# Channel statistics in three terms per chunk, two more blocks for ScalarE, and later pooled sums on GpSimd

## The chip, the cores and the metric

The kernel runs on one core of one Trainium2 chip. The metric is the device time of one execution in microseconds (us). TensorE is called PE, VectorE DVE, ScalarE ACT, GpSimd POOL; SP is the engine that only issues DMAs.

## The reference

The input x has 384 channels of 192 x 192 pixels, fp32. Two layers follow each other, each adding to x what it makes of the group-normalised x (32 groups of 12 channels):

```python
def _gn(v, G=32, eps=1e-5):
    g = v.reshape(B_, G, C_ // G, H_, W_)
    m = jnp.mean(g, axis=(2, 3, 4), keepdims=True)
    s = jnp.var(g, axis=(2, 3, 4), keepdims=True)
    return ((g - m) / jnp.sqrt(s + eps)).reshape(v.shape)

x = x + _L0_conv_ref(_gn(x), ...)   # 1x1 conv to q, k, v; 2x2 max; 3x3 depthwise;
                                    # channel attention; gelu; upsample by 2; 1x1 conv
x = x + _L1_conv_ref(_gn(x), ...)   # seven depthwise convs (13x13 and six smaller), each
                                    # with a batch norm, summed
```

The change concerns the first `_gn`: the mean and variance of each group of x, which must be known before the first 1x1 convolution can be finished.

## The kernel before

**Stages.** Channels are held as three chunks of 128 partitions (j = 0, 1, 2). The first stage, up to about 172 us, reads the whole of x once for its statistics. Then comes the main loop of 432 steps: `project` (L615, PE) multiplies a strip of x by the weights of one output chunk, `pool` takes the 2x2 maximum (L627 DVE, L634 ACT), and nine depthwise taps follow (L663 DVE). After it come the attention product with gelu, the second 1x1 convolution, and the large convolution (L1297).

**The statistics loop.** The first rows of all chunks arrive in the large tiles `xts` (read by L381 and L382). The rest of a chunk is cut into NX = 22 blocks of 128 x 1536 values (768 KB), and the loop runs over n = 22 j + b, 66 blocks in all, in a schedule written by hand (`manual_schedule`): within it each engine gets its instructions in the order in which the program issues them. A block is measured in one of two ways.

- By DVE: three `bn_stats` of 512 values (L476), each of which writes six numbers into `stats[:, j]`.
- By ACT, for the blocks b in BY_ACT = (4, 7, 10, 13, 16, 19) of chunks 0 and 1: the block plus a pivot with its sum (L472), and the square of that with its sum (L473), each followed by a short read of the accumulator. The pivot is the negative mean of the chunk's first block (L483, L484). The sums go to `acc`.

At the last block of a chunk (b = 21), after its L476, one `bn_aggr` (L505) makes mean and variance of all of the chunk's `stats`, and L510 to L515 do so for `acc`. Groups of 12 channels don't divide 128, so a few channels of the next chunk (`spares`) are measured as well (L502, L503) for chunks 0 and 1. Each of these results is a column of `mvx`; seven columns exist.

`group_stats` joins columns into groups: `mean_of` (L112) multiplies each column by its weight matrix `gw[k]` and adds up in PSUM, L123 spreads the group means back over the channels (one product for each term), L127 to L129 form the deviations, a second `mean_of` the variance, and L147 spreads scale and shift, which end up in `gn0`. It is a generator: with `apart` its steps are placed one by one between L476 instructions. It runs three times: `ga` for chunk 0 within chunk 1, `ge` for chunk 1 within chunk 2, and `g0` for chunk 2 after the loop.

**Loads.** Blocks land in a ring of eight buffers (eight more blocks, `kept`, have places of their own). `load_blocks` is called after each block: the buffer just read is given back and at once taken by the next block that waits, which is block n + 8 for n of 26 and more. It is issued from POOL if its number is odd and from SP if it is even:

```python
                eng = nc.scalar if n < 8 else nc.gpsimd if n % 2 == 1 else nc.sync
                eng.dma_start(out=xs, in_=x[j * P : (j + 1) * P, FX + b * FB : FX + (b + 1) * FB])
```

**Early products.** As soon as a chunk's `gn0` is known, PE starts on 18 products (EARLY). `first_chunk` advances by a step at each L476 of chunk 1, `early` at each L476 of chunk 2 until it first yields True (`going`). ACT prepares their input (`ready`, L387), copies results out of PSUM (`put_by`, L409) and earlier partial results back into PSUM (`fill`, L246). `early` first goes through `group_stats`, then, without a yield, through its entries 0 to 14, and yields at entry 15 and after. Each `ready` also appends its input to `early_sums`; `sum_one`, called at every odd n, makes POOL add up four pixels to one (L257 to L259) and store the result with a DMA (L261). What is left of `early_sums` is done after the loop, ahead of the main loop. There are 16 such sums.

`merge`, one step for each n, has POOL merge the convolution weights and prepare `gw`. L1029 to L1035, written after the main loop in a section of their own that runs partly beside it (they execute near 1607 us), combine columns of `mvx` into the input's variance `mv0` for the second normalisation.

Of the kernel before, what the change touches and what calls it, by code (L numbers as in the profile page):

```python
# [7 lines left out]
F32 = mybir.dt.float32  # L8
AF = mybir.ActivationFunctionType
ALU = mybir.AluOpType  # L10
AX = mybir.AxisListType
# [3 lines left out]
P = 128  # L15
# [5 lines left out]
NG = 32  # L21
# [36 lines left out]
def tile_attn_then_large_kernel_conv(ctx: ExitStack, tc: tile.TileContext, a: dict, out: bass.AP):  # L58
# [118 lines left out]
    mv0 = const.tile([P, NJ, 2], F32, name="mv0")  # L177


    mvx = const.tile([P, 7, 2], F32, name="mvx")  # L180
    BY_ACT = (4, 7, 10, 13, 16, 19)
    PART = len(BY_ACT) * R / HS
    PARTS = (1 - PART, PART)
    terms = [(0, NJ), (1, 0), (2, 0), (3, NJ + 1), (4, 1), (5, 1), (6, 2)]
    ctx_v, ctx_a, ctx_qk = ExitStack(), ExitStack(), ExitStack()
    vpool = ctx_v.enter_context(tc.tile_pool(name="vpool", bufs=1))
    v = vpool.tile([P, NJ, HS, WS], F32, name="v")
# [80 lines left out]
    with (  # L268
# [60 lines left out]
            out=wd[:, :nqk], in_=a["w_dw"][: nqk * P].rearrange("(m p) t -> p m t", p=P)  # L329
        )  # L330
        nc.gpsimd.dma_start(out=bdw[:, :nqk], in_=a["b_dw"][:, :nqk])
        gwt = s1.tile([P, 2 * NJ - 2, NG], F32, name="gw")
        gw = []
        for j in range(2):

            e = stats[:, j].rearrange("p n s -> p (n s)")
            gw += [e[:, -3 * NG : -2 * NG], gwt[:, 2 * j], gwt[:, 2 * j + 1]]
        gw.append(gm[:, 2])

        def merge():  # L340

            c0 = BC - 1
            for j in range(NJ):
                nc.gpsimd.tensor_scalar(wf[:, j, c0 : c0 + K0, :], wbs[0][:, j], scale[:, j, 0:1], None, ALU.mult)
                yield
                for i, (k, r) in enumerate(BRANCHES):
                    o = PAD - r * (k - 1) // 2
                    n = r * (k - 1) + 1
                    zv = wf[:, j, c0 + o : c0 + o + n : r, o : o + n : r]
                    wb = wbs[i + 1][:, j]  # L350
                    nc.gpsimd.tensor_scalar(wb, wb, scale[:, j, i + 1 : i + 2], None, ALU.mult)
                    nc.gpsimd.tensor_add(zv, zv, wb)
                    yield
                if j > 0:
                    continue
                for jj in range(2):
                    g = P * (jj + 1) // CG
                    nc.gpsimd.memset(gw[3 * jj], 0.0)
                    nc.gpsimd.memset(gw[3 * jj][:, g : g + 1], MORE[jj] / P / CG)
                    for q, part in enumerate(PARTS):  # L360
                        nc.gpsimd.tensor_scalar(gw[3 * jj + 1 + q], gm[:, jj], part, None, ALU.mult)
                    yield
                    k = P * (jj + 1) - 1
                    nc.gpsimd.tensor_copy(
                        gmt[:, C + jj * P : C + (jj + 1) * P], gmt[:, k : k + 1].to_broadcast([NG, P])
                    )
                    yield
# [42 lines left out]

        def first_chunk():

            pc = yield from group_stats(s1, s_ps, mvx, "ga", gw, terms[:3], (0,), True)
            yield
            nc.vector.tensor_copy(gn0[:, 0], pc[:, 0])
            yield
            blocks = sorted({B for B, _ in EARLY if B >= NKEEP})
            ready(blocks[0], 0, 0)
            for B, m in EARLY:
                if B < NKEEP:  # L420
                    continue
                ps = multiply(B, m, (0,))
                if m == 0 and B + 1 in blocks:
                    ready(B + 1, 0, 0)
                if m > 0 and B - NKEEP < 2 * NKEEP // (NJ - 1) and m < NJ:
                    n = (B - NKEEP) * (NJ - 1) + m - 1
                    ready(n // 2, n % 2, 0)
                put_by(B, m, ps)
                yield
                yield  # L430

        def early():

            pc = yield from group_stats(s1, s_ps, mvx, "ge", gw, terms[1:6], (1,), True)
            yield
            nc.vector.tensor_copy(gn0[:, 1], pc[:, 1])
            ready(0, 0, 1)
            ahead = None
            for n, (B, m) in enumerate(EARLY):
                if m == 0 and B < EARLY[-1][0]:  # L440
                    ready(B + 1, 0, 1)
                ps = multiply(B, m, (0, 1)) if B < NKEEP else multiply(B, m, (1,), ahead)
                if n + 1 < len(EARLY) and EARLY[n + 1][0] >= NKEEP:
                    fill(*EARLY[n + 1], 0)
                    ahead = filled.pop()
                if n == len(EARLY) - 1:
                    yield True
                put_by(B, m, ps)
                if n < NKEEP:
                    ready(n, 1, 1)  # L450
                if n >= len(EARLY) - LATE - 1:
                    yield True
# [5 lines left out]
        early_sums, pieces = [], {}  # L458
        begin, first = first_chunk(), early()
        going = False  # L460
        pivot = s1.tile([P, 2, 2], F32, name="pivot")
        acc = s1.tile([P, 2, len(BY_ACT), 2], F32, name="acc")
        done = [NS0] * NJ
        for n in range(NJ * NX):
            if n in (1, 3, 5, 7):
                rows_stats(n // 2)
            j, b = divmod(n, NX)
            xt = xss.pop(n)
            if j < 2 and b in BY_ACT:

                sums2 = acc[:, j, BY_ACT.index(b)]
                nc.scalar.activation(xt, xt, AF.Identity, bias=pivot[:, j, 0:1], accum_out=sums2[:, 0:1])  # L472
                nc.scalar.activation(xt, xt, AF.Square, accum_out=sums2[:, 1:2])  # L473
            else:
                for q in range(FB // 512):
                    nc.vector.bn_stats(stats[:, j, done[j], :], xt[:, q * 512 : (q + 1) * 512])  # L476
                    done[j] += 1
                    if j == 1:
                        next(begin, None)
                    if j == 2 and not going:  # L480
                        going = next(first)
                if j < 2 and b == 0:
                    nc.vector.bn_aggr(pivot[:, j], stats[:, j, NS0 : done[j]].rearrange("p n s -> p (n s)"))  # L483
                    nc.vector.tensor_scalar(pivot[:, j, 0:1], pivot[:, j, 0:1], -1.0, None, ALU.mult)  # L484
            if (j, b) not in kept:
# [1 line left out]
            for _ in load_blocks():  # L487
                pass
            next(merging, None)
            if n % 2 == 1:  # L490
                sum_one()
            if j < 2 and b == NX - 16:
                w = P * (j + 1)
# [4 lines left out]
            if j < 2 and b == NX - 6:  # L498
                k = HW * MORE[j] // P // 384
                sy = stats[:, j, -k:]  # L500
                for q in range(k):
                    nc.vector.bn_stats(sy[:, q, :], spares[j][:, q * 384 : (q + 1) * 384])  # L502
                nc.vector.bn_aggr(mvx[:, 3 * j, :], sy.rearrange("p n s -> p (n s)"))  # L503
            if b == NX - 1:
                nc.vector.bn_aggr(  # L505
                    mvx[:, (1, 4, 6)[j], :], stats[:, j, : done[j]].rearrange("p n s -> p (n s)")
                )
                if j < 2:
                    m = mvx[:, 3 * j + 2, :]
                    nc.vector.tensor_reduce(m, acc[:, j].rearrange("p n s -> p s n"), AX.X, ALU.add)  # L510
                    nc.vector.tensor_scalar(m, m, 1.0 / len(BY_ACT) / FB, None, ALU.mult)
                    t = s1.tile([P, 1], F32, name=f"sq{j}")
                    nc.vector.tensor_mul(t, m[:, 0:1], m[:, 0:1])
                    nc.vector.tensor_sub(m[:, 1:2], m[:, 1:2], t)
                    nc.vector.tensor_sub(m[:, 0:1], m[:, 0:1], pivot[:, j, 0:1])  # L515
        nc.sync.dma_start(out=wqk[:, 2, :C], in_=wqkv[:, 2, :C])
        nc.sync.dma_start(out=wqk[:, :, C:], in_=wqkv[:, :, C : 2 * C])
        nc.sync.dma_start(
            out=wfd.rearrange("(j p) s -> p j s", p=P), in_=wf.rearrange("p j x y -> p j (x y)")
        )  # L520
        last = group_stats(s1, s_ps, mvx, "g0", gw, terms[4:], (2,))
        for _ in range(5):
            next(last)
        next(first)
# [5 lines left out]
        normalize(0, 1, 2)  # L530
        next(first)
        assert next(first, first) is first


    mv1 = const.tile([P, NJ, 2], F32, name="mv1")
# [4 lines left out]
    with ctx_v:  # L540
# [362 lines left out]
        def gram_next():  # L903
            add_gram(*turned.pop(0))

        attention = []

        def begin_attention():
# [10 lines left out]
            for u in range(2 * NJ if B >= NB else 4 * NJ)  # L919
        ]  # L920
        with ctx_m:
            for sb in range(2):
                for j in range(NJ):
                    normalize(0, sb, j)
                    add_up(0, sb, j)
# [60 lines left out]
        with (  # L986
# [31 lines left out]
            with tc.manual_schedule():  # L1018
# [5 lines left out]
                nc.vector.tensor_mul(t, t, gn0[:, :, 1])  # L1024
                nc.vector.tensor_sub(pre[:, :, 0], bpj, t)
                nc.vector.memset(mv1, 1.0)

                d = b1.tile([P, 2, 1], F32, name="d")
                nc.vector.tensor_sub(d, mvx[:, 1:5:3, 0:1], mvx[:, 2:6:3, 0:1])  # L1029
                nc.vector.tensor_mul(d, d, d)  # L1030
                nc.vector.tensor_scalar(d, d, PART * (1 - PART), None, ALU.mult)
                for q, part in enumerate(PARTS):
                    nc.vector.scalar_tensor_tensor(d, mvx[:, q + 1 : q + 5 : 3, 1:2], part, d, ALU.mult, ALU.add)
                nc.vector.tensor_copy(mv0[:, :2, 1:2], d)
                nc.vector.tensor_copy(mv0[:, 2, 1:2], mvx[:, 6, 1:2])  # L1035
                hxs = [gather(b) for b in range(2)]
                sms = [load_sums(b) for b in range(2)]
                for c in range(NJ):
# [468 lines left out]
```

## Time and profile before

| | us |
|---|---|
| median of 3 runs (3071.37 to 3073.4) | 3073.17 |
| the profiled execution | 3071.29 |
| its span in the trace | 3069.2 |
| PE, DVE, ACT, POOL busy | 2934.8, 2516.2, 1336.9, 933.6 |
| first load to the first L615 | 0.75 to 174.68 |
| first block of chunk 0, 1, 2 begun by DVE | 11.59, 70.60, 121.42 |
| `gn0` written for chunk 0, 1, 2 | 78.23, 129.84, 172.07 |
| last block issued, landed, aggregated | 155.00, 163.18, 167.26 |
| main loop (first to last L615) | 174.68 to 1919.9 |

The page divides the span into 40 slices, gives the busy share of each engine in tenths, and follows the work that ended last back to the start (the chain of waits). In a timeline, a line gives the start, the busy time, the engine, the line of the program, the operation with output and input, the count, and in brackets how long the engine had been idle before it and what released it.

### The profile page before, as it was taken

What the parts mean: (1) busy time and instruction counts of PE and PEld (TensorE: products, weight loads), DVE (VectorE), ACT (ScalarE), POOL (GpSimd) and SP (SyncE); (2) the same over time, 40 slices, a digit from 0 to 9 for tenths busy, and PEclk for the clock granted to TensorE, in tenths of its full rate; (3) what the DMA queues carried; (4) which work ended last, traced back from release to release, by engine and by line L of the source; (5) the groups of instructions that cost most, each with busy time, mean ns of one, the idle gap of its engine ahead of it and who ended that gap; (6) DMA issues with size and microseconds to landing.
All of it is one profiled execution on the core that took longest, in us unless ns stands there. A gap on an engine that the chain in (4) does not pass through costs nothing.

```text
span 3069.2 us, 32213 instructions
## 1 busy us (share of the span) xinstructions
PE 2934.8 (96%) x10842; PEld 1943.7 (63%) x10842; DVE 2516.2 (82%) x3483; ACT 1336.9 (44%) x2457; POOL 933.6 (30%) x1147
## 2 busy tenths in 40 slices
PE   0699999999999999999999999999999999999998
PEld 0355556666666666665555555555777777777776
DVE  6778897888878787879999999888788777777775
ACT  2655554444444444444444444733333333333332
POOL 4422133232323242412222222500333333333332
PEclk9899999999999999999999999999999999999999
DMA  9943342434333333433333332577999999999994
GB/s 386 381 155 105 121 155 85 146 96 138 102 128 112 122 124 109 138 104 103 102 101 110 124 102 70 179 225 205 264 266 242 247 240 246 246 244 245 244 219 119
DMA packets 275924, 525.73 MB, mean 171 GB/s; under 512 B 25954, under 2 KB 190480, under 8 KB 275632
## 3 DMA queue, kind: packets, MB, share of 16 engines
q1 hardware_dynamic: 204432, 326.44, 39.8%
q0 software_dynamic: 49376, 174.29, 17.6%
q10 hardware_dynamic: 21952, 22.95, 2.2%
q8 instruction: 86, 1.41, 0.2%
q14 instruction: 78, 0.64, 0.1%
HBM read 362.23 MB, written 161.37 MB: 171 GB/s over the span
## 4 chain that ended last, share of the span: by engine, by line
PE 83%; DVE 10%; DMA 3%; issue 2%; ACT 1%; POOL 0%; ACTq 0%; SPq 0%; POOLq 0%; DVEq 0%
PE qkv L615 45%; PE conv L1297 29%; DVE v L663 3%; PE pj L1359 3%; DVE acc L663 2%; PE av L1051 2%; DVE mx L627 2%; PE gram L704 2%; PE tr L692 2%; DMA v<-in_x 1%; DMA xt<-in_x 1%; PE qkv L398 1%; DVE stats L476 1%; DMA smj<-sums 1%; DMA pd<-pjs 1%
## 5 line engine op out<-in xcount | busy, mean ns | idle before, releaser
L615 PE MATMUL qkv<-xt,wqk 128*128 128x384 f32 x3312 | 1088.6, 487 | 5.6 <-ACT qkv L246 5.1
L1297 PE MATMUL conv<-xp,wt 128*128 128x288 f32 (+1 forms) x3840 | 919.4, 403 | 2.2 <-ACT co L1305 2.2
L615 PEld LDWEIGHTS qkv<-xt,wqk 128*128 128x128 f32 x3312 | 621.6, 190 | 425.7 <-ACT qkv L246 11.5
L1297 PEld LDWEIGHTS conv<-xp,wt 128*128 128x128 f32 x3840 | 730.1, 190 | 189.2 <-ACT co L1305 2.6
L663 DVE SCALAR_TENSOR_TENSOR acc<-pooled,wd,acc 128x384 f32<-128x384 f32 (+2 forms) x1152 | 731.9, 635 | 30.6
L634 ACT ACTIVATE pooled<-mx,bq 128x192 f32<-128x192 f32 x432 | 197.1, 456 | 922.0 <-DVE mx L627 921.8
L627 DVE TENSOR_REDUCE mx<-qkv 128x192 f32<-128x768 f32 x432 | 412.3, 954 | 211.5 <-PE qkv L615 199.0
L1279 DVE STREAM_TRANSPOSE xp<-xn 128x4608 f32<-128x4608 f32 (+1 forms) x107 | 441.9, 4130 | 172.8 <-PE conv L1297 163.3
L615 PE MATMUL qkv<-xt,wv 128*128 128x384 f32 x1728 | 563.7, 487 | 1.7 <-ACT xt L596 1.1
L615 PEld LDWEIGHTS qkv<-xt,wv 128*128 128x128 f32 x1728 | 325.5, 190 | 234.4 <-ACT xt L596 7.5
L1305 ACT ACTIVATE co<-conv,cb 128x288 f32<-128x288 f32 x384 | 191.4, 499 | 602.4 <-PE conv L1297 592.1
L663 DVE SCALAR_TENSOR_TENSOR v<-pooled,wd,v 128x384 f32<-128x384 f32 (+2 forms) x576 | 375.7, 652 | 15.1
L257 POOL TENSOR_TENSOR sum<-xt 128x192 f32<-128x192 f32 x128 | 87.3, 682 | 957.0 <-ACT xt L596 944.4
L1322 POOL DMA_DIRECT2D out<-o x191 | 106.1, 585 | 571.7 <-DVE o L1313 514.1
L596 ACT ACTIVATE xt<-xt,gn 128x768 f32<-128x768 f32 x278 | 275.8, 1016 | 0.0
L1256 POOL TENSOR_TENSOR raw<-raw,up 128x2496 f32<-128x2496 f32 x46 | 230.9, 5019 | 23.3 <-DMA up<-pd 23.0
L1313 DVE STREAM_TRANSPOSE o<-co 128x2304 f32<-128x2304 f32 (+1 forms) x50 | 209.8, 4200 | 19.8 <-ACT co L1305 19.8
L732 POOL DMA_DIRECT2D zd<-v x96 | 72.2, 759 | 242.1 <-ACT v L723 241.4
L1359 PE MATMUL pj<-v,wp 128*128 128x384 f32 x432 | 142.5, 488 | 0.9 <-ACT gx L1062 0.6
L1359 PEld LDWEIGHTS pj<-v,wp 128*128 128x128 f32 x432 | 81.0, 190 | 55.5 <-ACT gx L1062 1.2
L258 POOL TENSOR_TENSOR sum<-sum,xt 128x192 f32<-128x192 f32 x128 | 100.9, 788 | 10.8
L1264 ACT ACTIVATE xn<-raw,par 128x2112 f32<-128x2112 f32 x48 | 102.9, 2143 | 1.2 <-ACT pjs L1367 1.2
(284 smaller groups left out, 1918.7 us busy)
## 6 DMA issues: line engine op xcount, KB each, us to landing
xt<-in_x SPq DMA_DIRECT2D x96, 1152.0 KB, 7.5
wt<-zd SPq DMA_DIRECT2D x46, 1536.0 KB, 13.4
raw<-in_x SPq DMA_DIRECT2D x182, 312.0 KB, 13.1
out<-o POOLq DMA_DIRECT2D x188, 288.0 KB, 6.7
zd<-v POOLq DMA_DIRECT2D x96, 416.0 KB, 4.6
up<-pd SPq DMA_DIRECT2D x184, 156.0 KB, 12.2
xs<-in_x POOLq DMA_DIRECT2D x20, 768.0 KB, 10.0
smj<-sums SPq DMA_DIRECT2D x72, 192.0 KB, 2.9
```

The source lines that it names most:

```text
L596: nc.scalar.activation(xt[:, j], xt[:, j], AF.Identity, bias=gn0[:, j, 1:2], scale=gn0[:, j, 0:1])
L615: nc.tensor.matmul(ps[:, r, : 2 * W], lhsT=wq[:, j, mm * P : (mm + 1) * P], rhs=xt[:, j, r * 2 * W : (r + 1) * 2 * W], start=(j == 0), sto ...
L627: nc.vector.tensor_reduce(mx, ps[:, :, : 2 * W].rearrange("p r (y w x) -> p r w y x", y=2, x=2), AX.XY, ALU.max,)
L634: nc.scalar.activation(pool_t[m][:, k : k + SR, 1 : 1 + WS], mx, AF.Identity, bias=bq[:, m : m + 1])
L663: nc.vector.scalar_tensor_tensor(acc[:, :nt], pool_t[m][:, k0 + dy : k0 + dy + nt, dx : dx + WS], wd[:, m, t : t + 1], acc[:, :nt], ALU.mu ...
L1256: eng.tensor_add(rv, rv, uv.unsqueeze(2).to_broadcast([P, (m1 - m0) * WS, 2]))
L1279: nc.vector.transpose(bass.AP(at.tensor, at.offset, [list(at.ap[0]), [NBQ, n], [1, NBQ], [NQ * NBQ, CC], [ME * NBQ, NE]],), bass.AP(row.te ...
L1297: nc.tensor.matmul(ps[:, t0:t1], lhsT=wt[:, c, o : o + P], rhs=d[:, c, g + 2 * t0 : g + 2 * t1 - 1 : 2, :], start=(g == 1), stop=(g == NGR ...
L1305: nc.scalar.activation(co[:, c], ps, AF.Identity, bias=cb[:, cc : cc + 1])
L1313: nc.vector.transpose(bass.AP(at.tensor, at.offset, [list(at.ap[0]), [2 * W, n], [BC, NBQ], [W, 2], [1, BC]]), bass.AP(of.tensor, of.offse ...
L1322: engines[u % len(engines)].dma_start(out=bass.AP(out.tensor, out.offset + k * CC * HW + (2 * u + t0 * BR) * W, [[ME * UQ * W, CC * NE], [ ...
L1359: nc.tensor.matmul(ps, lhsT=wp[:, j, i * P : (i + 1) * P], rhs=v[:, j, b * RB : (b + 1) * RB, :].rearrange("p r w -> p (r w)"), start=(j = ...
```

## The change

For each chunk the last block becomes a term of its own: at b = 21 the aggregate of all the blocks before is issued ahead of the last block's L476, with the small steps on `acc`, and after it a short aggregate over the last block alone. `mvx` has 11 columns, and the three calls of `group_stats` take 4, 7 and 6 terms where they took 3, 5 and 3. Chunk 2 gets two ACT blocks, b = 1 and b = 7, with a pivot of its own. `sum_one` is called in the loop only once `going` is true. `early` fills two entries ahead, after `put_by`, where it filled one ahead before it. `merge` makes nine weight matrices where it made four, and has two yields fewer; they lie in space that is otherwise unused. The input's variance is formed by twenty small DVE instructions, one in each of twenty steps of the main loop from step 108 on, in place of L1029 to L1035. The core of the diff:

```diff
-    mvx = const.tile([P, 7, 2], F32, name="mvx")
-    BY_ACT = (4, 7, 10, 13, 16, 19)
-    PART = len(BY_ACT) * R / HS
-    PARTS = (1 - PART, PART)
-    terms = [(0, NJ), (1, 0), (2, 0), (3, NJ + 1), (4, 1), (5, 1), (6, 2)]
+    mvx = const.tile([P, 11, 2], F32, name="mvx")
+    OF = (0, 4, 7)
+    BY_ACT = ((4, 7, 10, 13, 16, 19),) * 2 + ((1, 7),)
+    PARTS = [(1 - (len(bs) + 1) * R / HS, R / HS, len(bs) * R / HS) for bs in BY_ACT]
+    terms = [(OF[j] + q, j if q else NJ + j) for j in range(NJ) for q in range(j // 2, 4)]
...
+                for k, jj in terms:
+                    if jj < NJ:
+                        nc.gpsimd.tensor_scalar(gw[k], gm[:, jj], PARTS[jj][k - OF[jj] - 1], None, ALU.mult)
                 for jj in range(2):
...
-                    for q, part in enumerate(PARTS):
-                        nc.gpsimd.tensor_scalar(gw[3 * jj + 1 + q], gm[:, jj], part, None, ALU.mult)
-                    yield
...
-            pc = yield from group_stats(s1, s_ps, mvx, "ga", gw, terms[:3], (0,), True)
+            pc = yield from group_stats(s1, s_ps, mvx, "ga", gw, terms[:4], (0,), True)
...
-            pc = yield from group_stats(s1, s_ps, mvx, "ge", gw, terms[1:6], (1,), True)
+            pc = yield from group_stats(s1, s_ps, mvx, "ge", gw, terms[1:8], (1,), True)
...
-                ps = multiply(B, m, (0, 1)) if B < NKEEP else multiply(B, m, (1,), ahead)
-                if n + 1 < len(EARLY) and EARLY[n + 1][0] >= NKEEP:
+                ps = multiply(B, m, (0, 1)) if B < NKEEP else multiply(B, m, (1,), filled.pop(0))
+                if n + 1 == NKEEP * NJ:
                     fill(*EARLY[n + 1], 0)
-                    ahead = filled.pop()
                 if n == len(EARLY) - 1:
                     yield True
                 put_by(B, m, ps)
+                if NKEEP * NJ - 1 <= n < len(EARLY) - 2:
+                    fill(*EARLY[n + 2], 0)
...
-            if j < 2 and b in BY_ACT:
-
-                sums2 = acc[:, j, BY_ACT.index(b)]
+            if b == NX - 1:
+
+                n0 = done[j]
+                aggregate(j, 1, 0, n0)
+                na = len(BY_ACT[j])
+                m = mvx[:, OF[j] + 3, :]
+                nc.vector.tensor_reduce(m, acc[:, j, :na].rearrange("p n s -> p s n"), AX.X, ALU.add)
...
+            if b in BY_ACT[j]:
+
+                sums2 = acc[:, j, BY_ACT[j].index(b)]
                 nc.scalar.activation(xt, xt, AF.Identity, bias=pivot[:, j, 0:1], accum_out=sums2[:, 0:1])
                 nc.scalar.activation(xt, xt, AF.Square, accum_out=sums2[:, 1:2])
...
-                if j < 2 and b == 0:
+                if b == 0:
...
-            if n % 2 == 1:
+            if going and n % 2 == 1:
                 sum_one()
...
             if b == NX - 1:
-                nc.vector.bn_aggr(
-                    mvx[:, (1, 4, 6)[j], :], stats[:, j, : done[j]].rearrange("p n s -> p (n s)")
-                )
...
+                aggregate(j, 2, n0, done[j])
...
-        last = group_stats(s1, s_ps, mvx, "g0", gw, terms[4:], (2,))
+        last = group_stats(s1, s_ps, mvx, "g0", gw, terms[5:], (2,))
...
+        def input_variance():
...
+            for js in (slice(0, 2), slice(2, NJ)):
+                p, n = PARTS[js.start], js.stop - js.start
...
+                yield nc.vector.tensor_sub(d[:, js], mv[:, :, 2:4, 0], mv[:, :, 1:2, 0].to_broadcast([P, n, 2]))
...
+            variance = input_variance()
+            for s in range(2 * 10):
+                at(len(steps) // 4 + s, next, variance, None)
```

`aggregate(j, q, n0, n1)` is the `bn_aggr` of entries n0 to n1 of `stats[:, j]` into column OF[j] + q of `mvx`.

More of the change, by code (lines that the diff above doesn't have):

```diff
@@ L331, in tile_attn_then_large_kernel_conv @@
         nc.gpsimd.dma_start(out=bdw[:, :nqk], in_=a["b_dw"][:, :nqk])
-        gwt = s1.tile([P, 2 * NJ - 2, NG], F32, name="gw")
-        gw = []
-        for j in range(2):
+        gwt = s1.tile([P, 2, NG], F32, name="gw")
+        e = bn.rearrange("p j q i -> p (j q i)")
+        gw = [gwt[:, 0], gwt[:, 1], e[:, :NG], e[:, NG : 2 * NG]]
+        for j in range(NJ):
             e = stats[:, j].rearrange("p n s -> p (n s)")
-            gw += [e[:, -3 * NG : -2 * NG], gwt[:, 2 * j], gwt[:, 2 * j + 1]]
-        gw.append(gm[:, 2])
+            gw += [e[:, -36 - n * NG : -36 - (n - 1) * NG] for n in (1, 2)] if j < 2 else [e[:, -NG:]]
+        o = NJ * HS * WS - 2 * SR * WS
+        gw += [free[:, o - n * NG : o - (n - 1) * NG] for n in (1, 2)]
+        gw = dict(zip((k for k, _ in terms), gw))
         def merge():
@@ L355, in merge @@
                     continue
+                for k, jj in terms:
+                    if jj < NJ:
+                        nc.gpsimd.tensor_scalar(gw[k], gm[:, jj], PARTS[jj][k - OF[jj] - 1], None, ALU.mult)
                 for jj in range(2):
                     g = P * (jj + 1) // CG
-                    nc.gpsimd.memset(gw[3 * jj], 0.0)
-                    nc.gpsimd.memset(gw[3 * jj][:, g : g + 1], MORE[jj] / P / CG)
-                    for q, part in enumerate(PARTS):
-                        nc.gpsimd.tensor_scalar(gw[3 * jj + 1 + q], gm[:, jj], part, None, ALU.mult)
-                    yield
+                    nc.gpsimd.memset(gw[OF[jj]], 0.0)
+                    nc.gpsimd.memset(gw[OF[jj]][:, g : g + 1], MORE[jj] / P / CG)
                     k = P * (jj + 1) - 1
@@ L437, in early @@
             ready(0, 0, 1)
-            ahead = None
             for n, (B, m) in enumerate(EARLY):
@@ L460, in tile_attn_then_large_kernel_conv, with aggregate @@
         going = False
-        pivot = s1.tile([P, 2, 2], F32, name="pivot")
-        acc = s1.tile([P, 2, len(BY_ACT), 2], F32, name="acc")
+        pivot = s1.tile([P, NJ, 2], F32, name="pivot")
+        acc = s1.tile([P, NJ, len(BY_ACT[0]), 2], F32, name="acc")
+        def aggregate(j, q, n0, n1):
+            nc.vector.bn_aggr(mvx[:, OF[j] + q], stats[:, j, n0:n1].rearrange("p n s -> p (n s)"))
         done = [NS0] * NJ
@@ L468, in tile_attn_then_large_kernel_conv @@
             xt = xss.pop(n)
-            if j < 2 and b in BY_ACT:
-                sums2 = acc[:, j, BY_ACT.index(b)]
+            if b == NX - 1:
[4 more added lines that the diff above has]
+                nc.vector.tensor_reduce(m, acc[:, j, :na].rearrange("p n s -> p s n"), AX.X, ALU.add)
+                nc.vector.tensor_scalar(m, m, 1.0 / na / FB, None, ALU.mult)
+                t = s1.tile([P, 1], F32, name="sq")
+                nc.vector.tensor_mul(t, m[:, 0:1], m[:, 0:1])
+                nc.vector.tensor_sub(m[:, 1:2], m[:, 1:2], t)
+                nc.vector.tensor_sub(m[:, 0:1], m[:, 0:1], pivot[:, j, 0:1])
+            if b in BY_ACT[j]:
+                sums2 = acc[:, j, BY_ACT[j].index(b)]
                 nc.scalar.activation(xt, xt, AF.Identity, bias=pivot[:, j, 0:1], accum_out=sums2[:, 0:1])
@@ L502, in tile_attn_then_large_kernel_conv @@
                     nc.vector.bn_stats(sy[:, q, :], spares[j][:, q * 384 : (q + 1) * 384])
-                nc.vector.bn_aggr(mvx[:, 3 * j, :], sy.rearrange("p n s -> p (n s)"))
+                nc.vector.bn_aggr(mvx[:, OF[j], :], sy.rearrange("p n s -> p (n s)"))
             if b == NX - 1:
-                nc.vector.bn_aggr(
-                    mvx[:, (1, 4, 6)[j], :], stats[:, j, : done[j]].rearrange("p n s -> p (n s)")
-                )
[L508 to L515, printed above, removed]
+                aggregate(j, 2, n0, done[j])
         nc.sync.dma_start(out=wqk[:, 2, :C], in_=wqkv[:, 2, :C])
@@ L532, in tile_attn_then_large_kernel_conv @@
         assert next(first, first) is first
+        assert next(begin, begin) is begin
     mv1 = const.tile([P, NJ, 2], F32, name="mv1")
@@ L904, in gram_next @@
             add_gram(*turned.pop(0))
+        def input_variance():
+            d = aw.tile([P, NJ, 2], F32, name="d")
+            d2 = aw.tile([P, NJ, 2], F32, name="d2")
+            e = aw.tile([P, NJ, 1], F32, name="e")
+            for js in (slice(0, 2), slice(2, NJ)):
+                p, n = PARTS[js.start], js.stop - js.start
+                mv = mvx[:, OF[js.start] :][:, : 4 * n].rearrange("p (j q) s -> p j q s", q=4)
+                yield nc.vector.tensor_sub(d[:, js], mv[:, :, 2:4, 0], mv[:, :, 1:2, 0].to_broadcast([P, n, 2]))
+                yield nc.vector.tensor_mul(d2[:, js], d[:, js], d[:, js])
+                var = mv0[:, js, 1:2]
+                yield nc.vector.tensor_scalar(e[:, js], d[:, js, 0:1], p[1], None, ALU.mult)
+                yield nc.vector.scalar_tensor_tensor(
+                    e[:, js], d[:, js, 1:2], p[2], e[:, js], ALU.mult, ALU.add
+                )
+                yield nc.vector.tensor_mul(e[:, js], e[:, js], e[:, js])
+                yield nc.vector.scalar_tensor_tensor(
+                    var, mv[:, :, 1:2, 1], p[0], e[:, js], ALU.mult, ALU.subtract
+                )
+                for q in range(2):
+                    for t in (mv[:, :, 2 + q : 3 + q, 1], d2[:, js, q : q + 1]):
+                        yield nc.vector.scalar_tensor_tensor(var, t, p[1 + q], var, ALU.mult, ALU.add)
         attention = []
@@ L1026, in tile_attn_then_large_kernel_conv @@
                 nc.vector.memset(mv1, 1.0)
[L1028 to L1035, printed above, removed]
                 hxs = [gather(b) for b in range(2)]
```

## The prediction

> **What bounds the kernel now.** I read the page first, then the chain of waits from 112 to 180 us, then the timelines of ScalarE (ACT), GpSimd (POOL) and VectorE (DVE) there.
>
> ```profile
> PE 2934.8 (96%) x10842; PEld 1943.7 (63%) x10842; DVE 2516.2 (82%) x3483; ACT 1336.9 (44%) x2457; POOL 933.6 (30%) x1147
> ...
> PE   0699999999999999999999999999999999999998
> ...
> DMA  9943342434333333433333332577999999999994
> ```
>
> Only the first two slices (76.7 us each) leave TensorE (PE) free, and DMA is full there: the statistics stage, in which the whole change lies but for the variance steps. From then on PE has no hole, so **the start of L615 (174.7 us) is what can move the end**. Pieces of the chain before it:
>
> ```profile
> 155.00 8.16 DMA v<-in_x
> ...
> 163.18 1.89 DVE stats L476 x3
> ...
> 165.10 2.17 DVE mvx L505
> ...
> 167.77 0.84 PE g_pb L123 x6
> ...
> 174.89 5.23 PE qkv L615 x12
> ```
>
> The last block (n = 65), issued by POOL at 155.0, lands at 163.18; three L476, the aggregate L505, the group statistics and the last early products follow. Now ACT's timeline: start, middle and end of its early work.
>
> ```profile
> 130.00 1.95 ACT L387 ACTIVATE xt<-xt,gn 128x768 f32<-128x768 f32 x2 [2.67 <-DVE gn L436]
> ...
> 164.95 0.80 ACT L246 COPY qkv<-v 128x768 f32<-128x768 f32 x1
> 165.84 0.80 ACT L409 COPY v<-qkv 128x768 f32<-128x768 f32 x1
> 169.98 0.20 ACT L90 ACTIVATE g_r<-g_ve 32x1 f32<-32x1 f32 x1 [3.34 <-DVE g_ve L88]
> ```
>
> From 130.0 to 166.64 ACT works through what `early` issues for its entries 0 to 15, from 147 on without a pause. Once it has its group statistics, `early` doesn't yield before entry 15, so all of this enters ACT's queue at one place of the loop: after the ninth L476 of chunk 2. What a block behind such a queue costs is seen in chunk 1, first on ACT, then on POOL:
>
> ```profile
> 85.69 1.58 ACT L472 ACTIVATE v<-v,pivot 128x1536 f32<-128x1536 f32 x1
> 87.17 0.19 ACT L472 ACTIVATION_READ_ACCUMULATOR v<-v,pivot 128x1 f32 x1
> 87.40 1.48 ACT L473 ACTIVATE v<-v 128x1536 f32<-128x1536 f32 x1
> 88.79 0.19 ACT L473 ACTIVATION_READ_ACCUMULATOR v<-v 128x1 f32 x1
> ```
>
> ```profile
> 97.27 0.54 POOL L310 DMA_DIRECT2D xs<-in_x  x1 [7.67 <-ACT xs L473]
> ...
> 100.57 0.54 POOL L310 DMA_DIRECT2D xs<-in_x  x1
> ...
> 103.87 0.54 POOL L310 DMA_DIRECT2D v<-in_x  x1
> ```
>
> Block 26 had its pivot at 73.0 and ACT had nothing but a 0.2 us square root to do up to 78.4; it started at 85.69, after what `first_chunk` had queued before it. At 97.27 POOL had stood for 7.67 us before the load that takes an ACT block's buffer; the two loads behind it went out only then, 3.3 us apart, each with one sum between.
>
> **What the Trainium skill says.** "PSUM — Partial Sum Buffer", section "Engine vs sequencer instructions": ScalarE, VectorE and GpSimd queues are strict FIFO. The trace agrees (the 7.67 us). "SBUF — State Buffer", section "The DMA setup-cost knee": about 2 us plus bytes at 436 GB/s, 3.8 us for a 768 KB block. Here the shortest L310 took 4.3 us; I use that. "TensorE: Matmul & The Clock Gate", section "What's actually happening": an idle PE runs at half clock. The granted clock was 0.50 from 120 to 130 us, where a term of ge_pb took 0.46 us (2.29 / 5), against 0.27 for g_pb (0.82 / 3) straight after busy PE.
>
> **The change part by part.**
>
> *ScalarE's two blocks of chunk 2.* Blocks 1 and 7 are n = 45 and n = 51. The ninth L476 comes in block 46 now; without block 45 it comes in block 47. Block 45 is therefore queued on ACT ahead of `early`'s work, in the idle time between 118.6 and 127.1: 3.2 us (85.69 to 88.98), free. Block 51 is queued **behind** entry 15. Its buffer goes to load 59 (n + 8), which is odd and so POOL's, and loads 61, 63, 65 stand behind it. SP's loads 60, 62, 64 take buffers that DVE frees, and land early. The working:
>
> 1. First ready of `early`, now 130.0. Chunk 0 ends with one more small aggregate (0.24, as L483) and `ga` has a fourth term (0.4): ACT's chain of chunk 1, busy from 78.4 to 118.6 with short PE waits, shifts by 0.7. Chunk 1's small steps and last block follow ACT's end: 119.3 + 0.8 + 1.9 + 0.24 = 122.2 against 121.5. `ge` has two terms more, 2 x 0.46 = 0.9. The pivot (0.4) fits in the 1.2 us that DVE waited for ge_pb. Start: 131.6 (+1.6).
> 2. ACT's queue took 36.6 us; fill of entry 17 moves into it (0.8): ends at 169.0. Fills ahead of readies reorder a busy ACT: 0.
> 3. Block 51: 3.2, so 172.2. POOL issues load 59 at 172.5 (0.3 as at 97.27); it lands 4.3 later, 176.8. Until then DVE waits from about 148 on.
> 4. DVE takes blocks 59 to 64 at 1.79 each: 187.5. Loads 61, 63, 65, 3.3 us apart, land at 180.1, 183.4, 186.7, none late for DVE. Were they not behind load 59, this sum would be the same.
> 5. At n = 65 the long aggregate comes first: 390 of 444 elements of 2.16 us, 1.9; small steps 0.8 (69.89 to 70.68); L476 1.85; short aggregate 0.24: mvx is whole at 192.3, now 167.27, **+25.0**. The split of the aggregate saves nothing, since block 65 has landed by then.
> 6. `g0` has six terms for three, after an idle PE: pb 6 x 0.46 - 0.82 = +1.9; two means 3 terms each at 0.12 to 0.2, +0.6. **+2.5** (between 1.2 warm and 3.4 if entry 16's product, 1.83 us and ahead of g_pc, is at half clock).
>
> Sum: L615 starts +27.5 later, at 202.2.
>
> *Sums later.* Up to now POOL makes 8 sums in chunk 1 and issues loads 39, 41, 45, 47 and 49 about 3 us late for them. ACT bounds that stretch, so I count 0 (bounds -2 and 0). The sums still go one per odd n, 47 to 65, each three L257-L259 adds and an L261 issue (2.7 us). After load 65, five sums keep POOL to 197; the pooled memsets L578 need s1's space, free only after gn0, so they wait for nothing new. Six sums remain for the start of the main loop, beside a DVE with room (4.7 of 10 us busy from 180 to 190): 0, at worst +2, since PE lost 7.7 us to ACT and DVE later, between 200 and 410.
>
> *Merging.* Nine gw products for four, 5 x 0.29 = 1.5 us on POOL near 44 us, ahead of load 17; POOL idles before the following loads: 0, at worst +1 if the ring runs short.
>
> *Variance.* Twenty small DVE steps of 0.15 to 0.47 us, one per step from step 108 (near 600 us), where PE is 100% and DVE 81% busy: 0. Without that cover they cost up to 5. The eight removed at 1607 to 1611 lie under PE's L615: 0.
>
> The profiled execution took 3071.29 (span 3069.2 and 2.1 around it): 3071.29 + 27.5 = 3098.8. The median of the runs, 3073.17, is 1.9 higher; I forecast **3100**.
>
> **Rivals.** (A) *Not slower: block 51 isn't held.* It decides by whether ACT reaches block 51 before load 59 is needed, near 150 us. ACT's pauses while PE computes (130 to 147: 5 us and more) speak for room, a queue in the order of the program against it. Then the last block comes 1.7 us sooner (seven sums fewer ahead of it, 0.69 MB at the 415 GB/s of this stretch), the aggregate saves 2.16 - 0.24, `g0` costs 1.2 to 2.5: about -2, 3071; with the holes in DMA at 86 to 91 us (3 us) closed as well, 3066. (B) *Longer hold.* If loads 61 to 65 lag more than 5 us each behind sums that wait for their own DMA (3.65 us once, at 143), block 65 lands near 194, not 187; the long aggregate is then hidden: +31; with half clock +34, 3107. (C) *Shorter hold.* ACT's queue is 16 copies out, 11 in and 8 readies, 31 us without PE's waits, and PE limits its first half: at best 5 us less, 3095 down to 3090. The change does what it says in every case; I see no way for it not to.
>
> **How the numbers follow.** A measurement tells about 0.2% (6 us) from no change. Forecast 0.62, B 0.17, C 0.10, A 0.11, of which half is a gain over 6 us. So slower 0.89, same 0.05, faster 0.06. The range 3086 to 3111 takes the forecast with its bounds (23 to 34 us), B and C, and leaves A out.
>
> **What would show it.** Right: ACT's L472 and L473 of the seventh block of chunk 2 after the last L409 of the queue, near 169; POOL idle for over 25 us before one L310, released by ACT; DVE idle some 30 us before L476 and DMA nearly empty from 152 to 172; first L615 at 199 to 206; the same PE time after it. Wrong: L472 of chunk 2 before 150 us, a last landing before 165, or L615 starting by 176. If the start shifts and the end doesn't, the step that passes the delay on was wrong.

## The result, and the profile after

| | before | after |
|---|---|---|
| median of 4 runs each, one chip (us) | 3072.38 (3071.37 to 3073.4) | 3096.24 (3095.7 to 3097.61) |
| the profiled execution | 3071.29 | 3095.78 |
| its span | 3069.2 | 3094.0 |
| first ready of `early` | 130.00 | 128.41 |
| ACT through with its early queue | 166.64 | 167.3 |
| load of the last block issued | 155.00 | 180.67 |
| `mvx` of chunk 2 whole | 167.27 | 191.12 |
| first product of the main loop | 174.68 | 201.32 |

The kernel is slower by 23.9 us in the medians: ratio 1.0078, 95% interval 1.0061 to 1.0096. Lines have moved: the ready L387 is L390, `put_by`'s L409 is L412, ACT's pair L472 and L473 is L491 and L492, DVE's L476 is L495, the aggregate L505 is L468 (inside `aggregate`), the main loop's L615 is L625.

The page, its shares and its slices of 77 us each:

```profile
PE 2939.1 (95%) x10878; PEld 1947.7 (63%) x10878; DVE 2518.3 (81%) x3500; ACT 1342.5 (43%) x2465; POOL 934.8 (30%) x1152
...
PE   0669999999999999999999999999999999999998
...
DMA  9934424333342424233333332487999999999984
```

In PE's row one digit differs: the third slice's 9 has become a 6. Each engine's busy time is within 6 us of before, so most of the 24 us are not work but idle time. They lie ahead of the main loop. The chain of waits there (start, length, and what the time went to):

```profile
135.53 35.28 issue
170.83 4.44 DMA xs<-in_x
175.29 10.79 DVE stats L495 x18
186.10 1.92 DVE mvx L468
...
191.79 2.73 PE g_pb L123 x12
...
202.96 7.36 PE qkv L625 x22
```

Read from the top: a load is not issued for 35 us, lands 4.4 later, and six blocks' measurements, the long aggregate and the group statistics follow one after another. Who kept the load is seen in ACT's timeline (in brackets the idle time ahead, and who ended it):

```profile
128.41 1.95 ACT L390 ACTIVATE xt<-xt,gn 128x768 f32<-128x768 f32 x2 [2.68 <-DVE gn L439]
...
165.71 0.79 ACT L412 COPY v<-qkv 128x768 f32<-128x768 f32 x1
166.53 0.80 ACT L246 COPY qkv<-v 128x768 f32<-128x768 f32 x1
167.27 1.57 ACT L491 ACTIVATE xs<-xs,pivot 128x1536 f32<-128x1536 f32 x1
...
170.35 0.19 ACT L492 ACTIVATION_READ_ACCUMULATOR xs<-xs 128x1 f32 x1
...
196.35 0.20 ACT L90 ACTIVATE g_r<-g_ve 32x1 f32<-32x1 f32 x1 [25.81 <-DVE g_ve L88]
```

The first ready and the last copies of `early` are the two ends of one queue; block 51 stands behind it, and after it ACT has nothing to do for 25.81 us. POOL's timeline, the block's other side:

```profile
170.83 0.53 POOL L310 DMA_DIRECT2D xs<-in_x  x1 [35.30 <-ACT xs L492]
174.11 0.53 POOL L310 DMA_DIRECT2D xs<-in_x  x1
177.39 0.53 POOL L310 DMA_DIRECT2D xs<-in_x  x1
180.67 0.53 POOL L310 DMA_DIRECT2D v<-in_x  x1
```

The first is load 59, which takes block 51's buffer and waits 35.30 us for its L492; loads 61, 63 and 65 stand behind it on the same queue, 3.28 apart, each with one sum between. And DVE's:

```profile
175.29 8.99 DVE L495 BATCH_NORM_STATS2 stats<-xs 128x6 f32<-128x512 f32 x15 [29.12 <-DMA xs<-in_x]
...
186.10 1.92 DVE L468 BATCH_NORM_AGGREGATE mvx<-stats 128x2 f32<-128x390 f32 x1
...
190.88 0.24 DVE L468 BATCH_NORM_AGGREGATE mvx<-stats 128x2 f32<-128x18 f32 x1
```

DVE idles 29.12 us for load 59 and then meets no further wait: blocks 60 to 65 are there when it comes to them. The long aggregate sits between 186.10 and 188.02, in the open, since block 65 had landed before it (the DMA is quiet from 185 to 187).

### The profile page after: what moved, and what is told of

Its sections match the earlier page's. It is cut to its first block, busy times and chain, and to the rows that moved or that the text cites. A ratio compares the mean times of both kernels' runs of the same rounds, so it can differ in the third digit from the quotient of the medians.

```text
span 3094.0 us, 32302 instructions
## 1 busy us (share of the span) xinstructions
PE 2939.1 (95%) x10878; PEld 1947.7 (63%) x10878; DVE 2518.3 (81%) x3500; ACT 1342.5 (43%) x2465; POOL 934.8 (30%) x1152
## 4 chain that ended last, share of the span: by engine, by line
PE 83%; DVE 10%; DMA 3%; issue 3%; ACT 1%; POOL 0%; SPq 0%; ACTq 0%; POOLq 0%; DVEq 0%
PE qkv L625 44%; PE conv L1324 29%; PE pj L1386 4%; DVE v L673 3%; DVE acc L673 2%; PE av L1078 2%; DVE mx L637 2%; PE gram L714 2%; PE tr L702 2%; DVE stats L495 1%; DMA xt<-in_x 1%; DMA v<-in_x 1%; DMA pd<-pjs 0%; DMA xs<-in_x 0%; DVE xp L1306 0%
## 5 line engine op out<-in xcount | busy, mean ns | idle before, releaser
L625 PE MATMUL qkv<-xt,wqk 128*128 128x384 f32 x3312 | 1087.7, 487 | 6.3 <-ACT qkv L246 5.7
L625 PEld LDWEIGHTS qkv<-xt,wqk 128*128 128x128 f32 x3312 | 620.6, 190 | 426.2 <-ACT qkv L246 12.9
L637 DVE TENSOR_REDUCE mx<-qkv 128x192 f32<-128x768 f32 x432 | 412.1, 954 | 207.9 <-PE qkv L625 192.3
L625 PE MATMUL qkv<-xt,wv 128*128 128x384 f32 x1728 | 564.0, 487 | 1.7 <-ACT xt L606 1.1
L625 PEld LDWEIGHTS qkv<-xt,wv 128*128 128x128 f32 x1728 | 325.5, 190 | 234.7 <-ACT xt L606 7.8
```

The source lines that it names most:

```text
L625: nc.tensor.matmul(ps[:, r, : 2 * W], lhsT=wq[:, j, mm * P : (mm + 1) * P], rhs=xt[:, j, r * 2 * W : (r + 1) * 2 * W], start=(j == 0), sto ...
L637: nc.vector.tensor_reduce(mx, ps[:, :, : 2 * W].rearrange("p r (y w x) -> p r w y x", y=2, x=2), AX.XY, ALU.max,)
```

## The experiments

The theory, H: block 51 on ACT waits behind `early`'s copies, load 59 waits for its buffer, POOL's later loads stand behind that one, and DVE starves. Its rivals: the loss lies in the longer statistics (more terms, split aggregate) or in the later sums, or the hold is bounded by something other than ACT's place in the queue. The first four kernels are made from after; the times of before that belong to them have a median of 3072.37. Those that belong to the last four have 3071.27. A ratio is always to before, and an interval is at 95%.

**one_block: block 51 back to DVE, the rest of the change kept.**

```diff
-    BY_ACT = ((4, 7, 10, 13, 16, 19),) * 2 + ((1, 7),)
+    BY_ACT = ((4, 7, 10, 13, 16, 19),) * 2 + ((1,),)
...
```

What is left out of the diff moves a weight matrix of chunk 2 from the end of `stats`, where block 51's measurements now go, to a place of its own.

> ScalarE keeps block 1 of chunk 2 and gives block 7 back to VectorE; all else as after the change. Theory H (load 59 is held by a block queued behind `early`'s work): the hold is gone, POOL's longest wait before L310 in chunk 2 falls from 35 us to under 6, the last block lands before 162, ACT's queue (ends near 167) is then the last thing, L625 starts near 172 and the time is 3069 to 3072, 25 us less than after. Rival R (the extra terms, the reordered aggregate and the later sums cost the time): 3090 or more, since all of these stay.

Measured: 3069.77, ratio 0.9994 (0.9986 to 1.0002), not to be told from before. POOL's longest wait ahead of a load of chunk 2 is 5.29 us. DVE's timeline:

```profile
163.57 0.24 DVE L468 BATCH_NORM_AGGREGATE mvx<-stats 128x2 f32<-128x18 f32 x1
...
166.42 0.15 DVE L118 COPY g_mean<-g_ps 32x1 f32<-32x1 f32 x1 [2.61 <-PE g_ps L112]
```

`mvx` is whole at 163.8, 3.5 us sooner than before, and the next step then waits 2.61 us for PE, whose queue still holds the early products. The main loop starts at 175.50 and not near 172, 0.8 later than before, though the time is in the range expected. With one block fewer on ACT the whole loss is gone, so all of it hangs on block 51. The gain that the rest made at `mvx` is given back: from `mvx` to the main loop it takes 4.3 us more than before, of which 2.3 are this wait for PE, 0.7 the longer `g_pb` (1.49 for 0.82) and 1.0 the two early products that come with the group statistics (2.92 and 2.80 for 1.83 and 2.93).

**block14: the second ACT block is b = 14, whose buffer no later load takes.**

```diff
-    BY_ACT = ((4, 7, 10, 13, 16, 19),) * 2 + ((1, 7),)
+    BY_ACT = ((4, 7, 10, 13, 16, 19),) * 2 + ((1, 14),)
```

> ScalarE gets block 14 of chunk 2 in place of block 7: still queued behind `early`'s work, but no later load takes its buffer (n + 8 is beyond the last block). Theory H: no load is held, DVE measures all blocks but the last by 162; only the small steps on acc wait for ACT, to 170.6, then the last block and the short aggregate: mvx whole near 173.5, L625 near 183, time 3079 to 3082, a third of the loss. Rival Q (what costs is that the aggregate waits for ACT's late result, whichever block it is): as after, 3094 to 3098. If the buffer were all that matters: 3072.

Measured: 3078.67, ratio 1.0024 (1.0014 to 1.0035). The block is on ACT from 168.49 to 171.77, 1.2 us later than block 51 in after. DVE's timeline:

```profile
158.96 1.92 DVE L468 BATCH_NORM_AGGREGATE mvx<-stats 128x2 f32<-128x390 f32 x1
...
171.80 0.16 DVE L482 TENSOR_REDUCE mvx<-acc 128x2 f32<-128x4 f32 x1 [10.92 <-ACT v L492]
```

The same hold of ACT now keeps only the sums, 10.92 us of DVE, and no load: the first main-loop product starts at 184.88, 16.4 us sooner than in after. A late result alone thus costs 8.9 us against one_block (3078.67 - 3069.77), and the other 17.6 of after's loss against one_block come from the buffer. (The profiled execution, at 3082.61, is the slowest of seven, so the split is good to a few us.) Both kernels hold two blocks on ACT, so their number isn't the cause.

**block8: the second ACT block is b = 8, whose buffer goes to load 60 on SP.**

```diff
-    BY_ACT = ((4, 7, 10, 13, 16, 19),) * 2 + ((1, 7),)
+    BY_ACT = ((4, 7, 10, 13, 16, 19),) * 2 + ((1, 8),)
```

> ScalarE gets block 8 (n = 52) in place of block 7 (n = 51): the held load is 60, on SP's queue, with 62, 64 and the weight loads behind it; POOL's loads and sums run free. Theory H, in the form that DVE takes blocks in order so that one held load is enough: load 60 lands near 175.4, DVE has five blocks left and not six before the long aggregate, L625 about 1.8 us earlier than after, time 3093 to 3096. Rival P (the loss needs POOL's queue, where three loads stand behind the held one with a sum between each): 3080 to 3088.

Measured: 3095.25, ratio 1.0076 (1.0062 to 1.009). DVE's timeline:

```profile
174.37 7.22 DVE L495 BATCH_NORM_STATS2 stats<-xs 128x6 f32<-128x512 f32 x12 [25.89 <-DMA xs<-in_x]
```

With SP as the held queue and POOL free the time is the same as after's within the intervals, so POOL's queue and its sums are no part of the price. SP's loads 62 and 64 stand behind load 60 here, but in this trace as in after's DVE meets no further wait once the held block is there. What is paid for is the one late block, and DVE working through the blocks after it in order.

**split_early: both ACT blocks stay, but `early` yields ten times after its second entry,** so that its work enters ACT's queue in two parts, block 51 between them. (The sums start at block 47, as they did with `going`.)

```diff
+                if n == 1:
+                    for _ in range(10):
+                        yield
...
-            if going and n % 2 == 1:
+            if j == 2 and b >= 3 and n % 2 == 1:
```

> Blocks 1 and 7 stay with ScalarE; `early` yields ten times after its entry 1, so that block 7 enters ACT's queue after entry 1 and not after entry 15; the sums go at the same n as after. Theory H: block 51 is done by ACT near 141, load 59 leaves POOL near 142, DVE is through by 162; ACT's queue is 3.2 us longer than with one block and ends near 169 to 170, so L625 starts at 174 to 175 and the time is 3071 to 3074: no loss, but no gain from the second block. Rival R: 3090 or more. A gain of over 3 us against one_block would say that DVE, not ACT, ends last.

Measured: 3069.54, ratio 0.9993 (0.9985 to 1.0001). ACT's timeline, then POOL's:

```profile
138.13 1.56 ACT L494 ACTIVATE xs<-xs,pivot 128x1536 f32<-128x1536 f32 x1
```

```profile
141.69 0.53 POOL L310 DMA_DIRECT2D xs<-in_x  x1 [5.86 <-ACT xs L495]
```

Block 51 is on ACT 29 us sooner and load 59 goes out at 141.69, after a wait of 5.86 us for 35.30. The same work in another order loses nothing against before: the place in ACT's queue is the cause. Nor does the second block gain anything against one_block (3069.77).

**hold_alone: before, with nothing changed but block 51 on ACT.**

```diff
-            if j < 2 and b in BY_ACT:
+            if j < 2 and b in BY_ACT or n == 2 * NX + 7:
...
```

What is left out of the diff gives block 51's two sums a place of their own and takes the pivot of chunk 1.

> The kernel before with one edit: block 7 of chunk 2 (n = 51) goes to ScalarE's two passes in place of VectorE, with chunk 1's pivot. Their sums are not used, so the mean and variance of chunk 2 leave out that block. Nothing else of the change is in it. Theory H: ACT takes the block when `early`'s queue ends, near 166.7 to 169.9; load 59 leaves POOL near 170.2 and lands near 174.5; DVE has blocks 59 to 65 and the aggregate to go, 12.6 + 2.1, so mvx is whole near 189 (22 us later) and L615 starts near 198: time 3094 to 3097. Rival R (the three terms, later sums and merged weights carry part of the loss): 3080 to 3090, and the remainder is theirs.

Measured: 3095.45, ratio 1.0076 (1.0063 to 1.009), as after. POOL's timeline, then DVE's:

```profile
171.05 0.53 POOL L310 DMA_DIRECT2D xs<-in_x  x1 [31.86 <-ACT xs L474]
```

```profile
175.44 9.00 DVE L477 BATCH_NORM_STATS2 stats<-xs 128x6 f32<-128x512 f32 x15 [25.55 <-DMA xs<-in_x]
```

Load 59 leaves within 0.22 us of its time in after. Taken away, block 51's pass takes the whole loss with it (one_block); put in alone, it makes the whole loss. The loss needs neither the terms nor the split nor the later sums.

**sums_as_before: after, with the sums at every odd n again.**

```diff
-            if going and n % 2 == 1:
+            if n % 2 == 1:
```

> The kernel after with the sums back at every odd n from chunk 1 on. Theory H: the hold stays, so 3094 to 3099; chunk 1 is bound by ACT, so moving its sums back moves the first ready of `early` by no more than 1 us. Rival S (the later sums are what brought `early`'s start forward, 128.4 in place of the 131.6 of the prediction): first ready at 130.0 or later and time 3097 to 3100.

Measured: 3098.42, ratio 1.0089 (1.0074 to 1.0104). The first ready of `early` is at 129.41, 1.00 later than in after, and the first main-loop product at 202.56, 1.24 later. A gain by the later sums of this size isn't shown by it: the intervals of the times overlap with after's, and block14, which has the later sums and differs from after only behind this point, has its first ready at 129.92.

**sums_later_only: before, with the sums later and nothing else.**

```diff
-            if n % 2 == 1:
+            if going and n % 2 == 1:
```

> The kernel before with only the sums made later (`going` added to the condition). Loads 61, 63 and 65 no longer stand behind sums that wait for ACT, and some seven sums of DMA leave the stretch. Theory B (PE's and ACT's queue of `early`, which ends near 166, is the second bound right behind the data): the data are whole near 164, but g_ps stands on PE behind entry 15 until about 166, so L615 starts at 172.5 to 174 and the time is 3069 to 3072. Rival D (the data alone set it): L615 near 171 and 3068 or less.

Measured: 3066.57, ratio 0.9987 (0.998 to 0.9994). This version beats both kernels, before by some 4 us (1.8 to 6.1 by the interval). Theory B missed, and the numbers of rival D came. PE's timeline:

```profile
164.19 0.20 PE L112 MATMUL g_ps<-mvx,gm 128*32 128x1 f32 x2
164.63 0.82 PE L123 MATMUL g_pb<-g_mean,gmt 32*128 32x1 f32 x6 [0.24 <-DVE g_mean L118]
...
166.38 1.56 PE L398 MATMUL qkv<-v,wqk 128*128 128x384 f32 x4
...
171.27 28.98 PE L615 MATMUL qkv<-xt,wqk 128*128 128x384 f32 x87 [0.52 <-ACT qkv L246]
```

Load 65 goes out at 151.24 (before 155.00), `mvx` is whole at 164.0 (before 167.27), just as PE ends its queue, so that `g_ps` waits for nothing and PE keeps its clock: 0.82 us for the three terms, 1.56 for a product of entry 16. L615 starts 3.4 us sooner than before. (The profiled execution is the fastest of the 17, 2.6 us under their median; the rest of the 7.3 us between it and before's lies behind this start.)

1.95 of the 3.4 us are there at the first ready of `early`, 128.05 for 130.00. What sets it is seen in the chain of waits of before, and below it that of this version:

```profile
111.85 5.35 DMA xs<-in_x
...
117.22 1.89 DVE stats L476 x3
```

```profile
110.83 4.41 DMA xs<-in_x
```

The load is that of chunk 1's last block. In before DVE waits for it until 117.22, and ACT, through with the chunk at 118.59, is no longer waited for: L510 comes at 120.73. With the sums later the load goes out 1.02 us sooner and takes 0.94 us less, so DVE has the block at 115.26. The first part isn't due to the sums: in hold_alone, where they are as in before, the load goes out at 110.95. But there it lands after 6.51 us, and the first ready is at 130.30. So what the later sums take away in these traces is 0.9 to 2.1 us of this load's time.

With the rest of the change beside it, block 51 left out, the start is 4.2 us later (one_block: 175.50): more terms, slower products (2.92 and 2.80 for 1.56 each), and PE's queue ends 1.8 us later. Which of its parts makes PE's queue longer was not taken apart.

**late4: one_block with four products kept back for the time of the group statistics,** one ahead of `g_pc` and three after `gn0`, to free PE for `g_ps`.

```diff
-        LATE = 2
+        LATE = 4
...
```

What is left out of the diff is the edit of one_block, and two more calls of `next(first)` that place the products.

> one_block with LATE = 4 for 2, so that entries 14 to 17 and not 16 and 17 come after the statistics of chunk 2: one product between the variance and g_pc, the others after gn0. Theory B (in one_block the data were whole at 163.7, but g_ps waited 2.6 us on PE behind entry 15): g_ps goes at 163.8, the square root on ACT near 167.5, L625 starts near 173 and the time is 3067 to 3069.5, about 1 us below one_block. Rival: the four products only move from before to behind the statistics, PE has them to do either way, and L625 starts at 175 as in one_block.

Measured: 3072.86, ratio 1.0003 (0.9995 to 1.0011): a miss for the theory; the outcome is on the rival's side, with a start still later than its 175. PE's timeline:

```profile
164.53 2.72 PE L123 MATMUL g_pb<-g_mean,gmt 32*128 32x1 f32 x12 [0.24 <-DVE g_mean L118]
...
168.63 2.92 PE L401 MATMUL qkv<-v,wqk 128*128 128x384 f32 x4
...
178.73 21.61 PE L627 MATMUL qkv<-xt,wqk 128*128 128x384 f32 x65 [0.92 <-ACT qkv L246]
```

The 2.61 us wait is gone, `g_mean` comes 2.1 us sooner. But PE had then stood idle for 2.37 us, the clock granted from 164 to 174 was 0.50, and six terms took 2.72 us (1.49 in one_block); the products kept back did the rest.

## Why the prediction was right

The forecast was 3100 and slower; 3096.24 was measured, by the forecast's own mechanism. Step by step:

1. *First ready, 131.6:* 128.41, the only step with the wrong sign (-1.6 for +1.6). Two things were misjudged. Chunk 0 was put at +0.7 and the merging at 0 to +1; in fact chunk 0's first ready came 1.45 sooner, at 76.94 (before 78.39). The small aggregate and the fourth term cost 0.1 and 0.4 (0.24 and 0.4 predicted), but DVE could take block 20, whose load it waits for, at 62.61 and not at 64.61. The kernels made from after all have this ready at 76.84 to 77.25, those made from before at 78.33 and 78.44, and the sums don't matter for it: the change brings this load in 2 us sooner, and which part of it does so was not tried. The other is the later sums, below. The two terms more of `ge` cost 0.86 (0.9 predicted).
2. *ACT's queue, 37.4 long:* 38.9. Where ACT bounds, a cycle of three entries takes 5.75 us (156.79 to 162.54) for 5.63 (155.33 to 160.96): PE's wait for a fill is 0.92 where it was 0.80. Another 1.0 lies at the beginning: the first copy comes 5.32 us after the first ready, for 4.32 before, and the granted clock was 0.50 until about 134.0 for 133.2 before, though the products began sooner. The end, 169.0, came at 167.3.
3. *Block 51 3.2, load 59 at 172.5, landed 4.3 later:* 3.27, 170.83, 4.44.
4. *Six blocks to 187.5:* 10.79 us, to 186.08. Loads 3.3 us apart: 3.28. That their place behind load 59 doesn't matter was a remark of the forecast; DVE's timeline and block8 bear it out.
5. *`mvx` whole at +25.0:* +23.9, with 1.92 for the long aggregate, and the split saving nothing, as forecast.
6. *`g0` +2.5:* from `mvx` to the main loop it takes 2.8 more. The six terms took 2.72 (6 x 0.46 = 2.76 predicted).

The start at 201.32 is +26.6 for +27.5. That it is so near is luck in part: step 1 is off by -3.2 and step 2 by +1.5. That the end moves with the start, since PE has no hole after it, held nearly: the products of the main loop are 25.8 late in its middle (1348.6 became 1374.4) and 26.1 at the last one (1919.9 became 1946.0), the large convolution starts 24.8 late, and the span ends 24.8 late. 0.8 us come back at the first steps (148 products take 48.73 us for 49.49): before's L615 began at a granted clock of 0.50 (174 to 176), after's at 1.00 (200 to 202). Another 1.3 come back between the main loop and the large convolution, in the second 1x1 convolution's stage; that stretch takes 212.7 us in after and 214.0 in before, and 212.9 to 218.0 in other kernels' traces, though none of them changes it, so this is not more than the spread between executions.

What was put at nothing: the six late sums show no more than 0.6 us in PE's waits for ACT (5.7 for 5.1 in the first 260 us of the main loop). One thing was not foreseen: the pooled memsets L588 end at 204.1, and the first L637 on DVE waits for one of them (3.69 us), where before it waited for PE; PE's waits for DVE in that stretch stayed at 2.1 us. The variance steps show nowhere.

The signs named ahead were there: ACT's pair after the last copy, POOL idle over 25 us, DVE idle for 29, DMA nearly empty (2 GB/s from 160 to 170), PE's busy time nearly unchanged. Of the rivals, A (not held) is out by ACT's order, B (loads more than 5 apart) by the 3.28, C (a queue of 31 us) by the 38.9.

Beside chunk 0, the term that was mis-sized is *sums later*: the forecast took ACT to bound the stretch in which POOL issues loads 39 to 49 late, and counted 0, at best -2. In before that stretch ends with the load of chunk 1's last block, and ACT's sums are there 2.1 us ahead of their use. Alone the later sums bring some 4 us, outside that bound. In the change the split makes DVE take ACT's sums ahead of the last block, where it does wait for ACT (3.25 us before L482), and the two traces there differ by 1.0 us, which isn't clear of the spread.

## What to carry to other kernels

A block in a ring isn't priced by what its pass takes on an idle engine, but by when that engine's queue, in program order, reaches it, and by the next load that takes its buffer: 3.3 us of ACT's time cost 24 us here, and ten yields took all of it back. Before such a move, find what is issued in one piece ahead of it, and give the pass a block whose buffer nobody wants (6 us over before instead of 24) or a place ahead of the piece. Parts of a change should be tried singly: its cheapest one, a word in a condition, gained some 4 us alone (1.8 to 6.1) and was buried under the rest.

## What the runs showed of the hardware

PE's granted clock fell from 1.00 to 0.50 a few us after its last large product (128x384), and small products in between did not hold it up. The moment of the fall is read from windows of 0.25 us:

| kernel | last large product ends | PE after it | clock falls |
|---|---|---|---|
| after | 165.7 | idle from 166 to 188 | 168.2 |
| block8 | 165.3 | idle from 166 to 185 | 170.6 |
| late4 | 161.2 | busy for 0.07 of the 2 us from 162 to 164 | 163.8 |
| one_block | 165.9 | busy for 1.76 of the 2 us from 166 to 168 | 168.6 |
| split_early | 166.4 | busy for 1.76 of the 2 us from 166 to 168 | 171.2 |
| before | 165.8 | busy for 0.47 of the 2 us from 166 to 168 | 170.7 |

It takes 2.5 to 5.3 us, and no longer with PE busy on `g_ps` and `g_pb` than with PE idle. What decides within that range is not shown; in split_early and before a large product was running again when it fell. In sums_later_only, with 2.3 us between two large products (164.1 to 166.38), the clock stayed at 1.00. What it is worth: the product between the two halves of the group statistics took 2.92 us in one_block and late4, 1.83 in before and 1.56 in sums_later_only, and six terms of `g_pb` took 2.72 us in late4 and 1.49 in one_block, where the clock had not fallen yet. So a part of what one_block and late4 gained at `mvx` went to the clock.
